# Two attention layers with experts on one core: a reordered start, a later routing, loads and a mask bias moved at the turn between the layers

## The chip, the cores and the metric

The kernel runs on one core of a Trainium2 chip, in float32. Time is what the device takes for one launch, in microseconds (us). It has five engines with a queue of instructions each: TensorE (PE, matrix products and transposes; its loading of weights is listed as PEld), VectorE (DVE), ScalarE (ACT, functions from loaded tables, and copies), GpSimd (POOL) and SyncE (SP, which only issues transfers). Engines wait for each other by semaphores; an instruction that waits holds up all behind it in its own queue.

## The reference

Four batches of 512 rows of 256 values (x), each with a context of 1024 rows. Four steps change x in turn, each on the layer norm of x:

```python
x = x + L0_xattn(layernorm(x), ctx_1024, w_sim, b_sim, W_qv, b_qv)    # similarity attention
x = x + L0_ffn(layernorm(x), gate_w, expert_bias, w1, w2)             # 8 experts + 4 that return x, top 2
x = x + L1_xattn(layernorm(x), ctx_1024, mask, Wq, Wkv, Wo)           # 4 heads of 64
x = x + L1_ffn(layernorm(x), Wg, alpha, ln_w, ln_b, fc1, fc2)         # 8 experts, top 2
```

Layer 0's similarity of row i and context row j is x_i·w1 + c_j·w2 + (x_i·w3)·c_j + b. Its softmax over j weighs the context into one row for each x_i (`hq`); the softmax over i of the row maxima weighs x into one row of the batch (`hc`). The four blocks x, hq, x·hq, x·hc are multiplied by W_qv. An expert layer takes logits of each row, keeps the two largest, and adds the two experts' outputs with the softmax of the two logits as weights.

## The kernel before

**Stages.** Layer 0's attention goes batch by batch; then come the last routing, the keys and values of batches 0 and 1 for layer 1, layer 0's experts, the turn (expert outputs added to x, keys and values of batch 2, queries of batch 0), layer 1's attention in 32 units (four batches, four row tiles, two pairs of heads), and layer 1's experts. PE's order is written out by hand as the functions are called; SP's is so within the expert layers. VectorE, ScalarE and GpSimd get their order from a scheduler that takes priorities and dependencies; a dependency may be added by hand (`after`). Each buffer name belongs to a pool with a fixed number of slots (six of 8 KB, two larger ones, twelve of 4 KB), and a new user of a slot waits for the old.

**Loads (L130 to L169).** SP issues x_0, ctxT_0 (the transposed context), ctxn_0 (the plain one), W_qv, then x and ctxT of batches 1 to 3, then ctxn_1 to ctxn_3. Twelve small constants go by ACT's queue (`small`). Transfers rotate over eight semaphores, so that one waits for the eighth before it. After the last ctxT has landed, GpSimd issues zero fills of the rows and expert-output buffers in memory (L170 to L183, 20.6 MB).

**Layer 0's attention (L241 to L412).** `sim_prep` makes the layer norm of a batch, transposes it, scales it (`q0T`), multiplies it by a row vector (`junk`) and has GpSimd add a bias to x. `sim_scores` makes one row tile's scores, their maximum (VectorE) and exponentials (ScalarE). `turn_probs` divides and transposes the probabilities. `sim_finish` makes the attended product (L295), the reduced row and the product with W_qv, whose first four terms of `weff` close a batch. Into these the scores of the next batch are woven. `route_steps` routes a batch in four steps: norm and transposes, logits, the two largest and their counts (`pos`), then places, at which GpSimd scatters the rows to memory by eight indirect transfers (L753). The steps of batch b stand ahead of the next attended product.

**Layer 0's experts and the turn (L873 to L1031).** `tile_table` works out which expert each tile of 128 rows belongs to; 35 tiles read their rows, go through two products and are stored to `ys`. Then `layer0_experts` makes keys and values of batch 2, loads each batch's two expert outputs into 8 KB buffers (`yb`) and adds them to x on VectorE:

```python
    moe(L0, slots)
    sts[2] = mha_kv(2)
    for b in range(NB):
        y = t8([P, 2, NT, D], f"yb_{b}")
        ...
            nc.vector.tensor_tensor(x[b], y[:, k], x[b], ALU.add)
```

**Layer 1's attention (L418 to L595).** `mha_q` loads the mask of a batch, makes the norm, its transposes and the queries; for batch 0 it runs before the first unit, for the others it is woven into the units of the batch before. `mha_scores` makes the mask's bias (L478) at the first pair of heads of each row tile.

Of the kernel before, what the change touches and what calls it, by code (L numbers as in the profile page):

```python
# [8 lines left out]
F32 = mybir.dt.float32  # L9
# [8 lines left out]
P = 128  # L18
# [25 lines left out]

# [4 lines left out]
def two_layers(ctx: ExitStack, tc: tile.TileContext, io, out):  # L52
# [76 lines left out]

    def small(name, shape, src):  # L130
        t = const.tile(shape, F32, tag=name, name=name)
        nc.scalar.dma_start(out=t, in_=src)
        return t


# [8 lines left out]

    for b in range(NB):
        t = res.tile([P, NT, D], F32, tag=f"x{b}", name=f"x_{b}")
        nc.sync.dma_start(out=t, in_=io["x"][b].rearrange("(t p) d -> p t d", p=P))
        x.append(t)
        if b == 0:
            wsim = small("wsim", [P, 3, NC], io["w_sim"])  # L150
            bsim = small("bsim", [P, 1], io["b_sim"].partition_broadcast(P))
        t = res.tile([P, NC, M], F32, tag=f"ctxT{b}", name=f"ctxT_{b}")
        last_load = nc.sync.dma_start(out=t, in_=io["ctxT"][b].rearrange("(c p) m -> p c m", p=P))
        ctxT.append(t)
        if b == 0:
            load_ctxn(0)
            wqv = t8([P, 8, D], "wqv")
            nc.sync.dma_start(out=wqv, in_=io["W_qv"].rearrange("(k p) d -> p k d", p=P))
    bqv = small("bqv", [P, D], io["b_qv"].partition_broadcast(P))
    wsim_row = small("wsim_row", [P, D], io["w_sim_row"].partition_broadcast(P))  # L160
    gate_w = small("gate_w", [P, NC, ET0], io["gate_wT"].rearrange("(c p) e -> p c e", p=P))
# [23 lines left out]

    def layernorm(src, name):
        st = tsmall([P, NT, 6], "ln_st")
        mv = tsmall([P, NT, 2], "ln_mv")
        for t in range(NT):
            nc.vector.bn_stats(out=st[:, t, :], in_=src[:, t, :])  # L190
            nc.vector.bn_aggr(out=mv[:, t, :], in_=st[:, t, :])
        sd = tsmall([P, NT], "ln_sd")
        nc.scalar.activation(sd, mv[:, :, 1], AF.Sqrt, bias=eps)
        rs = tsmall([P, NT], "ln_rs")
        nc.vector.reciprocal(rs, sd)
        dst = t4([P, NT, D], name)
        for t in range(NT):
            nc.vector.tensor_scalar(
                dst[:, t, :], src[:, t, :], mv[:, t, 0:1], rs[:, t : t + 1], ALU.subtract, ALU.mult
            )  # L200
        return dst
# [38 lines left out]

    def sim_prep(b):  # L241
        xn = layernorm(x[b], f"xn0_{b}")
        eT = t4([P, NC, S], f"eT_{b}")
        qT = t4([P, NC, S], f"q0T_{b}")
        for c, pt in transposed(xn, f"eTp_{b}"):
            nc.vector.tensor_copy(eT[:, c, :], pt)
            nc.vector.tensor_scalar(  # L247
                qT[:, c, :], eT[:, c, :], wsim[:, 2, c : c + 1], wsim[:, 1, c : c + 1], ALU.mult, ALU.add
            )
        negmax = tsmall([P, NT], "s0_negmax")  # L250
        r = tsmall([P, NT], "s0_r")
        for t in range(NT):
            junk = t4([P, D], f"junk_{b}_{t}")
            nc.vector.tensor_tensor_reduce(
                junk, xn[:, t, :], wsim_row, 1.0, 0.0, ALU.mult, ALU.add, r[:, t : t + 1]
            )
        nc.gpsimd.tensor_tensor(x[b], x[b], bqv.unsqueeze(1).to_broadcast([P, NT, D]), ALU.add)
        return dict(b=b, xn=xn, eT=eT, qT=qT, negmax=negmax, r=r)

# [16 lines left out]
    def sim_finish(st):  # L276
# [15 lines left out]
        def attend(c):  # L292
# [5 lines left out]
            nc.scalar.copy(hq[:, c, :], op)  # L298
            nc.vector.tensor_tensor(eh[:, c, :], op, eT[:, c, :], ALU.mult)  # L299

# [59 lines left out]
    def layer0_attention():  # L360


        st, ps, routes = {0: sim_prep(0)}, {}, []

# [3 lines left out]
        def turns(b, t):  # L368
            if t == 0:
                st[b]["aT"] = tbig(f"a0T_{b}")  # L370
            turn_probs(st[b]["aT"], ps.pop(t), t, f"a0t_{b}_{t}")

        load_ctxn(1)
        scores(0, 0)
        scores(0, 1)
        turns(0, 0)
        scores(0, 2)
        turns(0, 1)
        scores(0, 3)
        st[1] = sim_prep(1)  # L380
        turns(0, 2)
        turns(0, 3)
        for b in range(NB):
            more = b + 1 < NB
            fin = sim_finish(st[b])
            next(fin)
            if more:
                scores(b + 1, 0)
            if routes:
                next(routes[-1])  # L390
            next(fin)
            if more:
                scores(b + 1, 1)
# [3 lines left out]
            next(fin)  # L397
            r = route_steps(L0, b)
            routes.append(r)
            next(r)  # L400
            if more:
                scores(b + 1, 2)
                turns(b + 1, 1)
                scores(b + 1, 3)
                if b + 2 < NB:
                    load_ctxn(b + 2)
                    st[b + 2] = sim_prep(b + 2)
                turns(b + 1, 2)
                next(r)
                next(r)  # L410
                turns(b + 1, 3)
                next(r)  # L412
        return r

# [3 lines left out]

    def mha_kv(b):

        kT = ctx_room(0, [P, NC, M], "kT_2") if b == 2 else t8([P, NC, M], f"kT_{b}")
        for n in range(NC):
            for h in range(2):
                op = mm_ps(f"k_{b}_{n}_{h}")
                for c in range(NC):
# [6 lines left out]
                else:  # L432
                    nc.vector.tensor_copy(kT[:, n, bass.ts(h, 512)], op)
        v = ctx_room(1, [P, NJ, D], "v_2") if b == 2 else t8([P, NJ, D], f"v_{b}")
        for g in range(NJ // 2):
            op = mm_ps(f"v_{b}_{g}")
            for k in range(2):
# [8 lines left out]
            else:  # L446
                nc.scalar.copy(d, op)
        return dict(b=b, kT=kT, v=v)

    def mha_q(st):  # L450
        b = st["b"]
        mask = t4([P, NT, M], f"mask_{b}", U8)
        nc.gpsimd.dma_start(out=mask, in_=io["mask"][b].rearrange("(t p) m -> p t m", p=P))
        xn = layernorm(x[b], f"xn2_{b}")
        yield
# [3 lines left out]
        for n in range(NC):  # L459
# [7 lines left out]
            else:  # L467
                nc.scalar.copy(qT[:, n, :], op)
        st.update(qT=qT, mask=mask)
        yield  # L470

    def mha_scores(st, n, t):

        b = st["b"]
        if n == 0:
            if t == 0:
                st["mbias"] = t8([P, NT, M], f"mbias_{b}", BF16)
            nc.vector.tensor_scalar(  # L478
                st["mbias"][:, t, :], st["mask"][:, t, :], 1.0, MASKED, ALU.subtract, ALU.mult
            )  # L480
        sps = [score_ps(f"s2_{b}_{n}_{t}_{r}") for r in range(2)]
# [9 lines left out]
        for r in range(2):  # L491
# [7 lines left out]
            ps.append(p)  # L499
        nc.vector.reciprocal(tot, tot)  # L500
        return ps, tot
# [49 lines left out]
    def layer1_attention(sts):  # L551
# [3 lines left out]
        units = []  # L555
        for _ in mha_q(sts[0]):
            pass
        for b in range(NB):
# [3 lines left out]
        for i in range(len(units) + 4):  # L562
# [22 lines left out]
            if b < NB and i % (2 * NT) == 2:  # L585
                queries = mha_q(sts[b] if b in sts else sts.setdefault(b, mha_kv(b)))
                next(queries)
# [94 lines left out]
    def route_steps(L, b):  # L682
# [49 lines left out]
        pos_i = tsmall([P, 2, NT], "rt_posi", I32)  # L732
        nc.vector.tensor_copy(pos_i, pos)  # L733
        wk = tsmall([P, 2, NT], "rt_wk")
# [30 lines left out]
        if L.n == 0:  # L765
            for t in range(NT):
                xs = x[b][:, t, :]
                nc.vector.scalar_tensor_tensor(xs, xn[:, t, :], wz[:, t : t + 1], xs, ALU.mult, ALU.add)
            yield
# [23 lines left out]
    def tile_table(L):  # L793
# [3 lines left out]
        n = tsmall([P, EX], "tt_n")  # L797
        nc.vector.tensor_tensor(n, lim, base[:, 0:EX], ALU.subtract)
        nc.vector.tensor_scalar(n, n, float(P - 1), None, ALU.add)
# [30 lines left out]
        dl = tsmall([P, EX], "tt_dl")  # L830
        nc.vector.tensor_tensor(dl[:, 0 : EX - 1], lim[:, 1:], lim[:, 0 : EX - 1], ALU.subtract)
        nc.vector.tensor_scalar(dl[:, EX - 1 :], lim[:, EX - 1 :], -1.0, None, ALU.mult)
        nc.vector.tensor_tensor(tmp, past, dl.unsqueeze(1).to_broadcast(big_shape), ALU.mult)
# [38 lines left out]

    def moe(L, slots):  # L873
        nf, n = L.nf, L.n
# [24 lines left out]
        def turn(i):  # L899
# [10 lines left out]
            if n == 0:  # L910
                nc.vector.tensor_copy(hT.rearrange("p c n -> p (c n)"), pt[:, 0:D])  # L911
            else:
# [59 lines left out]
        def run(lo, hi, at=None):  # L972
# [6 lines left out]
            for i in range(lo, hi + 1):  # L979
# [8 lines left out]
                if i > lo:  # L988
                    down(i - 1)
                    if i - 1 + RING < hi:  # L990
                        load_w(i - 1 + RING, 1)
                if i == at:
                    used.append(
# [19 lines left out]
    def layer0_experts(route):  # L1013

        slots = ring_slots(L0)
        sts = {0: mha_kv(0)}
        for _ in route:
            pass
        sts[1] = mha_kv(1)
        moe(L0, slots)  # L1020
        sts[2] = mha_kv(2)
        for b in range(NB):
            y = t8([P, 2, NT, D], f"yb_{b}")
            for k in range(2):
# [4 lines left out]
            for k in range(2):  # L1029
                nc.vector.tensor_tensor(x[b], y[:, k], x[b], ALU.add)  # L1030
        return sts  # L1031
# [82 lines left out]
```

## Time and profile before

| what | us |
|---|---|
| median of 5 runs (1034.93 to 1047.82) | 1045.27 |
| profiled execution, its own time | 1040.41 |
| its span, first to last instruction | 1038.5 |
| PE busy in the span | 916.3 |
| mean granted PE clock, share of full | 0.944 |

| stage | from, us | to, us | PE busy, us |
|---|---|---|---|
| loads and start of layer 0's attention | 0 | 48 | 25.9 |
| layer 0's attention, from the first attended product | 48 | 251 | 185.4 |
| last routing, keys and values of 0 and 1 | 251 | 290 | 33.8 |
| layer 0's experts | 290 | 400 | 106.3 |
| turn to layer 1 | 400 | 436 | 24.8 |
| layer 1's attention, its routing woven in | 436 | 750 | 278.0 |
| layer 1's experts | 750 | 1039 | 262.1 |

A line of the timeline has the start and the duration, the engine, the line of code, the operation, output and input, how often, and in brackets the idle time just before it with what ended it. A line of the waits has the total, the number of times and the longest. The slices cut the span in 40 equal parts and give the busy share of each in tenths. Engines work side by side; PE's gaps are where another engine or a transfer sets the pace.

### The profile page before, as it was taken

To read this page: it belongs to the slowest core of one execution; us is meant where nothing else is said; L and a number is where in the kernel's file an instruction comes from. 1 tells how busy PE (TensorE), PEld (TensorE's weight loads), DVE (VectorE), ACT (ScalarE), POOL (GpSimd) and SP (SyncE) were. 2 spreads that over 40 slices of the span, in tenths; PEclk is the share of its full clock that TensorE was granted. 3 is DMA by queue.
4 is the path that set the end of the run, shared out by engine and by line. 5 is a ranking of instruction groups with operands and counts; after the bars stand their busy time and mean duration, and the time that the engine had idled before them with its cause. 6 is when DMAs were issued, how large, how long until landed. Compare 5 with 4: busy or idle time off the path is not lost.

```text
span 1038.5 us, 15201 instructions
## 1 busy us (share of the span) xinstructions
PE 916.3 (88%) x5506; PEld 679.9 (65%) x5506; DVE 440.0 (42%) x1258; ACT 314.7 (30%) x714; POOL 224.8 (22%) x261
## 2 busy tenths in 40 slices
PE   4797989989899997799999789789669999999994
PEld 1445454646589985457656456566359999999993
DVE  4627466453622222766657256455521112111110
ACT  1212121121121110255655245455212323223230
POOL 2311120303312221010131230330622121222121
PEclk9899999999999998889999899889769999999997
DMA  8999900301068895100000101100624877678963
GB/s 286 303 221 250 272 15 1 110 4 68 28 222 265 247 327 177 66 21 2 21 1 6 56 21 42 41 21 2 258 89 105 253 239 236 178 244 263 305 210 97
DMA packets 55225, 144.65 MB, mean 139 GB/s; under 512 B 6454, under 2 KB 33133, under 8 KB 48968
## 3 DMA queue, kind: packets, MB, share of 16 engines
q1 hardware_dynamic: 37680, 103.90, 29.7%
q0 software_dynamic: 15344, 38.36, 15.1%
q10 hardware_dynamic: 2120, 1.35, 0.4%
q8 instruction: 46, 0.75, 0.3%
q14 instruction: 35, 0.29, 0.1%
HBM read 142.02 MB, written 42.14 MB: 177 GB/s over the span
## 4 chain that ended last, share of the span: by engine, by line
PE 43%; DVE 5%; issue 5%; ACT 3%; DMA 2%; POOL 1%; SPq 0%; POOLq 0%; ACTq 0%; DVEq 0%
PE hp L929 12%; PE y L950 11%; PE s L485 6%; PE a2t L508 4%; PE o L533 3%; DVE p L494 2%; ACT p L498 2%; PE q L462 1%; PE v L439 1%; PE k L426 1%; DMA acc<-yw,to 1%; PE wo L548 1%; DVE mbias L478 1%; ACT a2T L513 1%; POOL rowbuf L671 1%
## 5 line engine op out<-in xcount | busy, mean ns | idle before, releaser
L929 PEld LDWEIGHTS hp<-hT,w1s 128*128 128x128 f32 x1120 | 133.1, 195 | 3.7 <-DVE hT L915 1.9
L929 PE MATMUL hp<-hT,w1s 128*128 128x128 f32 x1120 | 133.7, 279 | 1.3 <-DVE hT L915 1.3
L938 ACT ACTIVATE aT<-hp,w1s 128x128 f32<-128x128 f32 x280 | 76.3, 383 | 168.4 <-issue 168.4
L950 PE MATMUL y<-w2s,aT 128*128 128x256 f32 x560 | 126.5, 379 | 0.0
L950 PEld LDWEIGHTS y<-w2s,aT 128*128 128x128 f32 x560 | 103.7, 190 | 12.7
L494 DVE CUSTOM_DVE_ANT_0 p<-s,mbias 128x1024 f32<-128x1024 f32 x64 | 75.8, 1221 | 71.7 <-PE s L485 71.7
L967 POOL DMA_INDIRECT acc<-yw,to x35 | 54.2, 1548 | 211.9 <-DVE to L902 126.9
L498 ACT ACTIVATE p<-p,s_nm 128x1024 f32<-128x1024 f32 x64 | 73.4, 1148 | 71.8 <-DVE s_nm L494 71.8
L508 PEld LDWEIGHTS a2t<-ident,p 128*128 128x128 f32 x512 | 58.3, 146 | 53.5 <-issue 34.3
L508 PE MATMUL a2t<-ident,p 128*128 128x128 f32 x512 | 73.6, 288 | 19.8 <-issue 12.2
L753 POOL DMA_INDIRECT rows<-rowbuf,rt_posi x64 | 63.2, 988 | 123.0 <-DVE rt_posi L733 88.0
L954 DVE TENSOR_SCALAR yw<-y,row 128x256 f32<-128x256 f32 x63 | 30.5, 484 | 135.2 <-PE y L950 135.2
L485 PE MATMUL s<-kT,q2T 64*128 64x512 f32 x256 | 72.3, 667 | 1.4 <-DVE s_nm L494 1.4
L915 DVE TENSOR_SCALAR hT<-ht,w1s 128x128 f32<-128x128 f32 x70 | 25.5, 406 | 95.1 <-PE ht L909 88.8
L533 PE MATMUL o<-a2T,v 128*64 128x128 f32 x1024 | 63.3, 276 | 0.0
L530 POOL COPY s_rs<-s_tot 128x128 f32<-128x128 f32 x32 | 9.8, 307 | 237.6 <-DVE s_tot L500 171.6
L533 PEld LDWEIGHTS o<-a2T,v 128*64 128x64 f32 x1024 | 55.4, 137 | 7.9 <-issue 7.3
L265 PE MATMUL s<-ctxT,q0T 128*128 128x512 f32 x128 | 59.2, 607 | 1.4 <-DVE q0T L247 1.4
L295 PE MATMUL hq<-a0T,ctxn 128*128 128x512 f32 x128 | 58.2, 609 | 0.9 <-DVE ehT L299 0.9
L513 ACT COPY a2T<-a2t 128x512 f32<-128x512 f32 x96 | 53.0, 582 | 15.7 <-PE a2t L508 14.5
L929 PEld LDWEIGHTS hp<-hT,w0s 128*128 128x128 f32 x448 | 54.3, 192 | 3.2 <-DVE hT L911 1.8
L929 PE MATMUL hp<-hT,w0s 128*128 128x128 f32 x448 | 54.7, 275 | 1.4 <-DVE hT L911 1.4
(222 smaller groups left out, 1205.8 us busy)
## 6 DMA issues: line engine op xcount, KB each, us to landing
w1s<-in_w1p SPq DMA_DIRECT2D x38, 1030.0 KB
w2s<-in_w2p SPq DMA_DIRECT2D x38, 1024.0 KB
rows<-zeros POOLq DMA_DIRECT2D x8, 2064.0 KB
w0s<-in_w1p SPq DMA_DIRECT2D x31, 512.0 KB
w0s<-in_w2p SPq DMA_DIRECT2D x31, 512.0 KB
row<-rows SPq DMA_DIRECT2D x63, 129.0 KB
ctxT<-in_ctxT SPq DMA_DIRECT2D x4, 1024.0 KB
ctxn<-in_ctx SPq DMA_DIRECT2D x4, 1024.0 KB
```

The costliest lines, as they stand in the source:

```text
L265: nc.tensor.matmul(sp[:, h, :], st["qT"][:, c, bass.ts(t, P)], ctxT[b][:, c, bass.ts(h, 512)], start=(c == 0), stop=(c == NC - 1),)
L295: nc.tensor.matmul(op, ctxn[b][:, j, bass.ts(c, P)], aT[:, j, :], start=(j == 0), stop=(j == NJ - 1))
L485: nc.tensor.matmul(sps[r][:, k, :], st["qT"][at, n, bass.ts(t, P)], st["kT"][at, n, bass.ts(k, 512)], start=True, stop=True,)
L494: nc.vector.tensor_tensor_reduce(p, sps[r].rearrange("p h n -> p (h n)"), st["mbias"][:, t, :], -ATT_SCALE, -ATT_SCALE * LEAST, ALU.add, A ...
L498: nc.scalar.activation(p, p, AF.Exp, bias=nm, scale=-1.0, accum_out=tot[:, r : r + 1])
L508: nc.tensor.transpose(pt[:, bass.ts(j, P)], p[:, bass.ts(4 * g + j, P)], ident)
L513: nc.scalar.copy(d, pt)
L533: nc.tensor.matmul(op[r * HD : r * HD + HD, :], st["v"][:, j, bass.ts(2 * n + r, HD)], aT[:, r, bass.ts(j, P)], start=(j == 0), stop=(j == ...
L753: i = nc.gpsimd.indirect_dma_start(out=rows[:, :], out_offset=bass.IndirectOffsetOnAxis(ap=pos_i[:, k, t : t + 1], axis=0), in_=buf[:, k, ...
L929: nc.tensor.matmul(o, w1[:, c * ff + f * P : c * ff + f * P + P], hT[:, c, :], start=(c == 0), stop=(c == NC - 1),)
L938: nc.scalar.activation(aT[:, f, :], hp[:, f // 4, bass.ts(f % 4, P)], AF.Gelu_apprx_tanh, bias=w1[:, at : at + 1])
L950: nc.tensor.matmul(op, aT[:, f, :], w2[:, f * D : f * D + D], start=(f == 0), stop=(f == nf - 1))
```

## The change

It has five parts.

1. The start. A square root of a constant is run on ScalarE ahead of all, which loads its table. Only two small loads stay on ACT's queue, two go to GpSimd's, and eight to SP's, behind the last ctxT and ahead of ctxn_1 to ctxn_3. SP's order becomes x_0, ctxT_0, x_1, ctxn_0, W_qv, ctxT_1, and so on.
2. `sim_prep` is cut in three: the norm, the transposes with the scaling, the products with the row vector. The norm of batch 1 is put behind batch 0's scaling, those of 2 and 3 behind the attended product two batches before.
3. The routing of a batch is taken one batch later, step by step among the next batch's products. Batch 3's is woven into the keys and values of 0 and 1 by `AMONG`: so many parts of these ahead of each step. The x updates and the tile table are put behind the places.
4. The mask of batch 0 is loaded ahead of layer 0's experts, and its four biases are made among their tiles, from the eighth on.
5. At the turn all eight expert outputs are loaded into the two large buffers. x_0's adds stay on VectorE, behind the last key copy of batch 2; the other six go to GpSimd. Queries of batch 0 come in the code right after x_0's adds. The norms of the other batches are put behind a unit's reciprocal.

```diff
+AMONG = (2, 1, 1, 2, 0)
...
-    def small(name, shape, src):
+    def small(name, shape, src, queue=nc.sync):
         t = const.tile(shape, F32, tag=name, name=name)
-        nc.scalar.dma_start(out=t, in_=src)
+        queue.dma_start(out=t, in_=src)
         return t
+    nc.scalar.activation(const.tile([P, 1], F32, tag="root", name="root"), eps, AF.Sqrt, bias=eps)
...
+    load_x(0)
+    wsim = small("wsim", [P, 3, NC], io["w_sim"], nc.scalar)
+    bsim = small("bsim", [P, 1], io["b_sim"].partition_broadcast(P), nc.scalar)
+    bqv = small("bqv", [P, D], io["b_qv"].partition_broadcast(P), nc.gpsimd)
+    wsim_row = small("wsim_row", [P, D], io["w_sim_row"].partition_broadcast(P), nc.gpsimd)
+    load_ctxT(0)
+    load_x(1)
+    load_ctxn(0)
+    wqv = t8([P, 8, D], "wqv")
+    nc.sync.dma_start(out=wqv, in_=io["W_qv"].rearrange("(k p) d -> p k d", p=P))
+    load_ctxT(1)
+    for b in range(2, NB):
+        load_x(b)
+        last_load = load_ctxT(b)
...
-    def layernorm(src, name):
+    def layernorm(src, name, behind=None):
...
-            nc.vector.bn_stats(out=st[:, t, :], in_=src[:, t, :])
+            i = nc.vector.bn_stats(out=st[:, t, :], in_=src[:, t, :])
+            if behind is not None:
+                after(i, behind, "a transfer does not hold up what VectorE has to do before")
...
+    def sim_norm(b, behind=None):
+        return dict(b=b, xn=layernorm(x[b], f"xn0_{b}", behind))
...
         for b in range(NB):
             more = b + 1 < NB
             fin = sim_finish(st[b])
             next(fin)
+            if b + 2 < NB:
+                st[b + 2] = sim_norm(b + 2, st[b]["attended"])
+            step()
             if more:
                 scores(b + 1, 0)
-            if routes:
-                next(routes[-1])
             next(fin)
+            step()
             if more:
                 scores(b + 1, 1)
             next(fin)
             if more:
                 turns(b + 1, 0)
             next(fin)
-            r = route_steps(L0, b)
-            routes.append(r)
-            next(r)
+            step()
             if more:
+                sim_rows(st[b + 1])
                 scores(b + 1, 2)
                 turns(b + 1, 1)
                 scores(b + 1, 3)
                 if b + 2 < NB:
                     load_ctxn(b + 2)
-                    st[b + 2] = sim_prep(b + 2)
+                    sim_prep(st[b + 2])
+            step()
+            if more:
                 turns(b + 1, 2)
-                next(r)
-                next(r)
                 turns(b + 1, 3)
-                next(r)
-        return r
+            route = route_steps(L0, b)
+            next(route)
+        return route
...
-        sts = {0: mha_kv(0)}
-        for _ in route:
+        mask = mha_mask(0)
+        def biases():
+            for t in range(NT):
+                after(mha_bias(sts[0], t), L0.turned, "a transfer does not hold up the tiles")
+                yield
+        sts = {}
+        kvs = mha_kvs(sts, (0, 1))
+        for n in AMONG:
+            for _ in range(n):
+                next(kvs)
+            next(route, None)
+        for _ in kvs:
             pass
-        sts[1] = mha_kv(1)
-        moe(L0, slots)
-        sts[2] = mha_kv(2)
+        sts[0]["mask"] = mask
+        moe(L0, slots, biases())
+        for _ in mha_kvs(sts, (2,)):
+            pass
         for b in range(NB):
-            y = t8([P, 2, NT, D], f"yb_{b}")
+            if b % 2 == 0:
+                yb = tbig(f"yb_{b}").rearrange("p (b k t) (w d) -> p b k (t w) d", b=2, k=2, d=D)
+            y = yb[:, b % 2]
...
             for k in range(2):
-                nc.vector.tensor_tensor(x[b], y[:, k], x[b], ALU.add)
+                if b == 0:
+                    i = nc.vector.tensor_tensor(x[b], y[:, k], x[b], ALU.add)
+                    after(i, sts[2]["copied"], "a transfer does not hold up the copies of the keys")
+                else:
+                    nc.gpsimd.tensor_tensor(x[b], y[:, k], x[b], ALU.add)
+            if b == 0:
+                for _ in mha_q(sts[0]):
+                    pass
```

## The prediction

> **What bounds the kernel now.** I read the page's busy shares and slices first, then PE's idle by stage, then the rows at each gap, last the chain of waits.
>
> ```profile
> PE 916.3 (88%) x5506; PEld 679.9 (65%) x5506; DVE 440.0 (42%) x1258; ACT 314.7 (30%) x714; POOL 224.8 (22%) x261
> PE   4797989989899997799999789789669999999994
> DVE  4627466453622222766657256455521112111110
> ```
>
> PE sets the pace in nearly all slices, so only PE's gaps can be won. By stage (PE busy of length): 25.9 of 48 us before the first attended product, 185.4 of 203 in layer 0's attention, 33.8 of 39 in the last routing, 106.3 of 110 in layer 0's experts, 24.8 of 36 at the turn to layer 1, 278 of 314 in layer 1's attention, 262 of 289 in its experts. The change edits the first five and hardly the last two.
>
> What holds PE at the start (waits, then rows of ACT and VectorE, then of PE):
>
> ```profile
> PE eTp L208 <- DVE xn L198: 17.5, 4, 13.7
> DVE ln_st L190 <- DMA x<-in_x: 8.1, 2, 5.0
> ```
> ```profile
> 10.73 0.48 ACTq L132 DMA_DIRECT2D wo<-in_Wo  x1
> 11.30 1.28 ACT L193 ACT_TABLE_LOAD   x1 [11.30 <-DMA alpha<-in_alpha]
> 12.60 0.30 ACT L193 ACTIVATE ln_sd<-ln_mv,eps 128x4 f32<-128x4 f32 x1
> ```
> ```profile
> 22.74 0.75 DVE L190 BATCH_NORM_STATS2 ln_st<-x 128x6 f32<-128x256 f32 x2 [3.07 <-DMA x<-in_x]
> 24.95 2.40 DVE L271 TENSOR_REDUCE s_negmax<-s 128x1 f32<-128x1024 f32 x2
> ```
>
> x_0's statistics are done at 6.7, but the square root waits until ACT has issued its 12 loads (to 11.2) and loaded its table. Later VectorE stands before x_1, while the first scores (ready from 21) wait for their maximum.
>
> At the last routing and the turn PE waits as follows:
>
> ```profile
> 272.53 0.42 PE L719 MATMUL pos<-rt_cnt,before 128*128 128x48 f32 x2 [3.19 <-DVE rt_cnt L711]
> ...
> 411.19 3.78 PE L426 MATMUL k<-ctxT,wkv 128*128 128x512 f32 x4 [5.00 <-DVE kT L433]
> 414.77 7.99 PE L439 MATMUL v<-wkv,ctxT 128*128 128x256 f32 x32
> 428.14 2.30 PE L208 MATMUL xn2Tp<-ident,xn 128*128 128x128 f32 x8 [5.38 <-DVE xn L198]
> 430.38 5.33 PE L462 MATMUL q<-xn2T,wq 128*128 128x512 f32 x8
> 435.63 1.99 PE L485 MATMUL s<-kT,q2T 64*128 64x512 f32 x8
> ```
>
> There eight adds of 1.22 us stand in VectorE's queue: the first (409.31) ahead of a key copy that PE needs, the others ahead of query 0's norm.
>
> **Part by part.** *Start.* With two small loads left on ACT and the table loaded beforehand, the root can follow the statistics: 6.7 instead of 12.6, so 5.9 earlier; xn and the first transposes move by as much (13.7 to about 7.9). The score matmuls then need ctxT_0, the second load in either order. VectorE no longer stops at x_1: the wait is put behind batch 0's scaling, and x_1 is issued third, without the stop at 11.16. PE has 3.8 us of gaps at transposes of batch 1 (2.23, 0.75, 0.81), of which I count 2. The first attended product moves from 48.2 to about 40: **−8**. Better end −12 (5.9, all 3.8 and the 2.4 of PE's wait for the first probabilities); worse −5, if the cold clock and later waits take the gaps back (the same 16 score matmuls took 8.79 first and 7.03 later).
>
> *Middle (48 to 251).* The table loads stay as many per batch here; what moves is routing. From a batch's reduced product to the next attended one takes 29.5, 28.4 and 24.9 us. In the first PE stands 2.65 + 0.66 + 0.35 + 0.68 + 0.29 = 4.6 us, the first two for the next norm, which now is made during the attended product, where VectorE waits anyway (21 us idle ahead of L299 from 100 to 260). Batch 0's routing work (2.23 transposes, 2.58 logits, 0.41 back, slow clock) leaves it: about −6.5, the gaps shrinking by only 1.3 because VectorE then has eT, q0T, probabilities and a0T copies in a row. Batch 1: −4.2 (3.3 of routing at full clock, 0.9 of gaps); batch 2: −1.8, since VectorE's four x updates now stand ahead of its last copy (about 1.6). The routing comes back in the next batch's attended stretch: 3.3 less the 1.1 of gaps that it fills (0.35 + 0.77 before the reduced product) is +2.1 twice, and +1.1 in batch 3, where 0.8 of counting moves out. Sum **−7**, from −12 (all the norm's gaps) to 0 (VectorE paces PE).
>
> *Last routing.* Batch 2's count now stands here too, and behind hcq_3 its top-2 has little PE work to hide it: a gap like the 3.19 above, some 4.5 with the logits' copies. Against it, batch 3's same gap is filled by K/V of batch 1. Scatters of 3 (8 at 1.28 on POOL) start when its places are ready, about 24 us behind hcq_3 as now, and batch 2's 8 (10.2 us) have gone before. First expert tile **+2.3** (−2 if K/V covers both, +5 if the clock also falls).
>
> *Experts of layer 0.* Four mask biases of 0.68 go among tiles of 3.7 us on a VectorE with 30.5 of 110 us busy; the mask keeps one small buffer of twelve. **+0.5** (0 to +4; the upper end is a tile's wait for a buffer).
>
> *Turn.* The first yb lands at 409.3 as now; x_0's two adds then end at 411.8, the norm (four statistics 1.7, root 0.3, table 1.28, xn 1.38) by about 416. PE has keys without the 5.0 gap until 407.8 and values until 415.8, so the transposes start near 416, queries near 418.3, scores near 423.7 instead of 435.63: −12, and I take **−11.5**. All eight yb loads still take SP's queue 12.5 us, but x_1 to x_3 are off the path for units of 6.5 us. The six adds on POOL (2.35 each by the 128x1024 row) are 14 us on an engine with 1.8 of 36 busy. They can collide:
>
> ```profile
> 15.82 1.42 DVE L247 TENSOR_SCALAR q0T<-eT,wsim 128x512 f32<-128x512 f32 x1
> ...
> 18.10 0.54 DVE L247 TENSOR_SCALAR q0T<-eT,wsim 128x512 f32<-128x512 f32 x1
> ```
>
> The first ran beside POOL's 128x1024 add (14.61 to 16.96), the second alone. If xn's four likewise take 2.6 times 1.38, it is +2.2: end −8 with a second such copy; other end −14 (no clock loss).
>
> The Trainium skill, "SBUF — State Buffer", section "Who interferes with whom", speaks against this move: GpSimd and VectorE share one port pair, and one of the two blocks for the other's whole instruction. The two rows agree. By the rule a copy could wait out a whole add, a little more than 2.35 us; the sum would be 1.2 us worse than with the 1.42 row.
>
> *Layer 1's attention.* The norms of 1 to 3 are put behind a unit's reciprocal, which by the built program means ten more table loads in the whole. Six to eight lie here, at
>
> ```profile
> 24.84 1.28 ACT L222 ACT_TABLE_LOAD   x1
> 26.18 1.11 ACT L222 ACTIVATE p<-s,s_negmax 128x1024 f32<-128x1024 f32 x1
> ```
>
> 1.28 + 0.06 us each, about 10 us of ACT, in units of which ACT fills half (155.9 of 314). I count a quarter as seen by PE: **+2.5** (0 to +8). The Trainium skill, "ScalarE: Activation LUTs", section "What ACT_TABLE_LOAD costs", has 1.28 plus a drain, 2.66 us a switch; here the next activation follows 0.06 after the load, so this trace shows no drain behind it. By the rule the same quarter would be +5.
>
> **The sum.** −8 −7 +2.3 +0.5 −11.5 +2.5 = −21.2. From the profiled run's own 1040.4 (span 1038.5 and 1.9 around it) that is 1019; from the median 1045.3, which is 4.9 above it, 1024. The profiled run is an ordinary one of the spread (1034.9 to 1047.8), so I say **1022**. Layer 1's experts (750 to 1040) keep order and work.
>
> **Rivals.** *Gain at the turn alone.* If in layer 0 VectorE (102 of 203 us busy, bunched in each batch's second half) becomes PE's bound, starting sooner only means waiting later: −8 + 5 + 2 − 11.5 + 3 = about −9, time 1034. For it: PE's gaps in the middle name VectorE. Against: VectorE is half idle there.
>
> *The turn's adds collide.* POOL's adds slow x_0's norm and first copies: turn −5 rather than −11.5, sum −15, time 1028.
>
> *Starved context loads: slower.* The SP queue now has eight small loads ahead of three contexts, all behind ctxT_3, whose landing releases 20.6 MB of zero fills on POOL's queue. Before, the third context was issued late:
>
> ```profile
> 22.80 45.24 SPq L142 DMA_DIRECT2D ctxn<-in_ctx  x3
> ```
>
> It was issued at 68, moved 0.06 MB by 75, then 0.25 MB per 5 us until 95: 27 us for 1 MB beside fills. Batch 1's attended product (near 84 now) needs context 1. Up to 4 MB at 50 GB/s from about 29 end at 109, context 1 at about 70, batch 2's by 90 (needed near 135). It decides if the rate falls below about 35 GB/s: at half the 50, context 1 lands near 110, PE stands 26 us and the sum is +5; with nothing until the fills end (about 120) it is +15. Time 1048 to 1058. For it: that 7 us with 0.06 MB. Against: 0.25 MB per 5 us after it.
>
> *It doesn't do what it says*: the gaps stay because another wait ends last at the same place (ctxT_0's landing at the start, yb's at the turn); about −3, time 1041.
>
> **How the numbers follow.** Forecast (−13 to −32) 0.68; gain at the turn alone 0.14; collision 0.07; starved 0.07; not as said 0.04. Range 1009 to 1038: the low end has the middle's and the start's better ends with the sum's others, the high end takes in the first two rivals and the worse ends of middle and layer 1. A measurement here tells about 1%, 10.5 us: faster 0.68 + 0.06 + 0.06 = 0.80; within 1% 0.13 (rest of those two, and the last); slower 0.07.
>
> **What would show it.** Right: the first root at about 6.8, first attended product near 40; fewer than 2 us at transposes per batch; no 5.0 gap in kT and scores about 24 us after the last expert product instead of 36. Wrong: PE waiting for ctxn in batch 1 or 2; a gap over 5 us before counting; xn of query 0 over 3 us; more PE idle in units with a table load; first tile over 5 us later behind hcq_3.

## The result, and the profile after

The changed kernel takes 1042.1 us (median of 44 runs) against 1041.6 for the kernel before (86 runs); the ratio is 1.0002, 95% interval 0.999 to 1.0014. No change can be seen, where 2% less was forecast. The start did move, and most of what it won was lost again before layer 1's attention began.

The page of the changed kernel, its busy shares and two of its slices:

```profile
PE 923.0 (88%) x5506; PEld 683.4 (65%) x5506; DVE 441.1 (42%) x1252; ACT 328.1 (31%) x725; POOL 240.5 (23%) x269
PE   5888989898898999689889799799669999999994
DVE  6454563725623223565656356456531111211110
```

PE is busier at once (5 and three 8s for 4, 7, 9, 7), and no busier afterwards. By stages, in us. They are split at the small product that stands right ahead of the first attended one, at the end of the last product with W_qv, at the first expert tile's transposes, at the end of the last expert product, at the first score, and at the end of layer 1's last attention output. The last columns are g_all, the repaired kernel of the third group below; each column is one traced run, and g_all's is from another chip:

| stage | before | predicted step | after | step | repaired | step |
|---|---|---|---|---|---|---|
| to the first attended product | 48.1 | −8 | 39.5 | −8.6 | 38.8 | −9.3 |
| rest of layer 0's attention | 203.1 | −7 | 206.9 | +3.8 | 197.1 | −6.0 |
| last routing to first expert tile | 38.1 | +2.3 | 42.0 | +3.9 | 39.7 | +1.6 |
| layer 0's experts | 110.2 | +0.5 | 112.8 | +2.6 | 110.4 | +0.2 |
| turn, to the first score | 36.0 | −11.5 | 31.9 | −4.1 | 21.7 | −14.3 |
| layer 1's attention, to its last output | 298.0 | +2.5 | 304.8 | +6.8 | 303.0 | +5.0 |
| the rest of the span | 304.9 | 0 | 305.9 | +1.0 | 305.4 | +0.5 |
| span | 1038.5 | −21.2 | 1043.8 | +5.3 | 1016.1 | −22.4 |

The profiled run of after is 3.6 us above its median (1045.6 with what stands around the span), that of before 1.2 below its own; the stages say where time went, and the medians how much in all.

PE's rows at the start, at the weights of batch 0 and of batch 1, and at the last routing (start, duration, what, and in brackets the idle time before with its releaser):

```profile
7.61 2.21 PE L223 MATMUL eTp<-ident,xn 128*128 128x128 f32 x8 [7.61 <-DVE xn L213]
...
39.70 8.36 PE L317 MATMUL hq<-a0T,ctxn 128*128 128x512 f32 x16
...
74.30 2.93 PE L353 MATMUL hcq<-weff,eT 128*128 128x256 f32 x6 [3.20 <-DVE weff L371]
...
131.05 0.98 PE L365 MATMUL hcc<-ones,b_hr 1*128 1x1 f32 x4 [2.53 <-DVE a0T L251]
...
250.59 0.66 PE L771 MATMUL pos<-rt_cnt,before 128*128 128x48 f32 x2 [3.87 <-DVE rt_cnt L763]
...
284.84 3.72 PE L475 MATMUL v<-wkv,ctxT 128*128 128x256 f32 x16 [2.14 <-DVE v L481]
```

The first transposes come at 7.61 (13.70 before), the first attended product at 39.70 (48.23): the start is as forecast. The gaps at 74.30, 131.05 and 284.84 are new. Behind them stand these rows: of VectorE at weff (the kernel before, then after) with GpSimd's beside it, of ACT at the exponential of batch 2's second row tile, of VectorE at the first tiles' row numbers.

```profile
78.65 0.88 DVE L349 SCALAR_TENSOR_TENSOR weff<-wqv,b_hc 128x256 f32<-128x256 f32 x2
```
```profile
69.87 4.38 DVE L371 SCALAR_TENSOR_TENSOR weff<-wqv,b_hc 128x256 f32<-128x256 f32 x2
69.92 1.65 POOL L192 DMA_DIRECT2D ys<-zeros  x1 [20.56 <-issue]
71.51 2.42 POOL L268 TENSOR_TENSOR x<-x,bqv 128x1024 f32<-128x1024 f32 x1
```
```profile
128.00 1.11 ACT L237 ACTIVATE p<-s,s_negmax 128x1024 f32<-128x1024 f32 x1 [10.70 <-DMA ys<-zeros]
```
```profile
283.97 0.22 DVE L958 SCALAR_TENSOR_TENSOR to<-row,tt_valid,tt_aside 128x1 int32<-128x1 f32 x1 [3.98 <-DMA row<-rows]
284.10 0.69 DVE L481 COPY v<-v 128x512 f32<-128x512 f32 x1
```

Two steps of weff took 0.88 us before and 4.38 now: GpSimd issued the fill of ys from 69.92 and added to x_2 from 71.51 to 73.93. The exponential waits for the zero fills to end: they read a constant tile of zeros out of a 4 KB buffer, and that buffer is the one that the exponential is given. And the copy of values that PE needs stands behind a row number whose row is still on its way.

The turn (PE, then VectorE's norm of query 0 before and after, then GpSimd):

```profile
402.54 7.10 PE L461 MATMUL k<-ctxT,wkv 128*128 128x512 f32 x16 [1.32 <-PEq L1063]
409.49 7.30 PE L475 MATMUL v<-wkv,ctxT 128*128 128x256 f32 x32
419.15 0.33 PE L223 MATMUL xn2Tp<-ident,xn 128*128 128x128 f32 x1 [2.37 <-DVE xn L213]
421.50 0.48 PE L223 MATMUL xn2Tp<-ident,xn 128*128 128x128 f32 x1 [2.02 <-DVE xn L213]
423.92 0.47 PE L223 MATMUL xn2Tp<-ident,xn 128*128 128x128 f32 x1 [1.94 <-DVE xn L213]
426.27 1.33 PE L223 MATMUL xn2Tp<-ident,xn 128*128 128x128 f32 x5 [1.87 <-DVE xn L213]
```
```profile
427.67 1.38 DVE L198 TENSOR_SCALAR xn<-x,ln_mv,ln_rs 128x256 f32<-128x256 f32 x4
```
```profile
417.04 9.17 DVE L213 TENSOR_SCALAR xn<-x,ln_mv,ln_rs 128x256 f32<-128x256 f32 x4
```
```profile
414.18 14.31 POOL L1107 TENSOR_TENSOR x<-yb,x 128x1024 f32<-128x1024 f32 x6 [11.18 <-DMA yb<-ys]
```

The gap of 5.0 in the keys is gone, as forecast. But the four steps of xn, 1.38 us before, take 9.17 beside the six adds that went to GpSimd, and PE gets its four row tiles some 2.4 us apart, one for each add.

### The profile page after: what moved, and what is told of

Its sections match the earlier page's. It is cut to its first block, busy times and chain, and to the rows that moved or that the text cites. A ratio compares the mean times of both kernels' runs of the same rounds, so it can differ in the third digit from the quotient of the medians.

```text
span 1043.8 us, 15228 instructions
## 1 busy us (share of the span) xinstructions
PE 923.0 (88%) x5506; PEld 683.4 (65%) x5506; DVE 441.1 (42%) x1252; ACT 328.1 (31%) x725; POOL 240.5 (23%) x269
## 4 chain that ended last, share of the span: by engine, by line
PE 61%; issue 11%; DVE 10%; DMA 8%; ACT 4%; POOL 4%; another core or an unknown queue 1%; SPq 0%; POOLq 0%; DVEq 0%; ACTq 0%
PE hp L985 11%; PE y L1006 10%; PE s L536 6%; PE hq L317 6%; PE s L287 5%; DMA acc<-yw,to 5%; PE a2t L559 4%; PE hcq L353 4%; PE o L584 3%; DVE p L545 2%; ACT p L549 2%; DMA row<-rows 1%; POOL rows L805 1%; POOL ys L1013 1%
## 5 line engine op out<-in xcount | busy, mean ns | idle before, releaser
L559 PEld LDWEIGHTS a2t<-ident,p 128*128 128x128 f32 x512 | 58.7, 147 | 55.4 <-issue 32.5
L536 PE MATMUL s<-kT,q2T 64*128 64x512 f32 x256 | 75.7, 695 | 1.4 <-DVE s_nm L545 1.4
L317 PE MATMUL hq<-a0T,ctxn 128*128 128x512 f32 x128 | 60.3, 627 | 0.0
```

Of the source, the lines that this page charges most:

```text
L317: nc.tensor.matmul(op, ctxn[b][:, j, bass.ts(c, P)], aT[:, j, :], start=(j == 0), stop=(j == NJ - 1))
L536: nc.tensor.matmul(sps[r][:, k, :], st["qT"][at, n, bass.ts(t, P)], st["kT"][at, n, bass.ts(k, 512)], start=True, stop=True,)
L559: nc.tensor.transpose(pt[:, bass.ts(j, P)], p[:, bass.ts(4 * g + j, P)], ident)
```

## The experiments

The runs came in three groups ("calls" in the recorded expectations), each on one chip. The kernel before takes between 1027 and 1041 us on these chips, so a ratio is compared only with those of its own group.

**First group: repair one collision at a time.** The four kernels are the changed one with these edits:

```diff
 f_turn: the adds of x_1 to x_3 behind query 0's norm
-                    nc.gpsimd.tensor_tensor(x[b], y[:, k], x[b], ALU.add)
+                    i = nc.gpsimd.tensor_tensor(x[b], y[:, k], x[b], ALU.add)
+                    after(i, normed["last"], "the first norm goes before")
 f_weff: the fill of ys and the add to x_{b+2} behind batch b's weff
+        after(late_fill["ys"], behind, "the product's weights go before")
+        if behind is not None:
+            after(i, behind, "the product's weights go before")
 f_zeros: the zeros in their own buffer (room for it from one shared in time with oT)
-    zeros = t4([P, ROW], "zeros")
+    zeros = const.tile([P, ROW], F32, tag="zeros", name="zeros")
 f_all: all of these, and the first two tiles' row numbers behind batch 1's values
+            if n == 0 and i < 2:
+                after(k, hold, "the values go before")
```

> The changed kernel, with the six adds on GpSimd put behind the last tile of query 0's norm. Theory (the adds shut VectorE out): xn of query 0 falls from 9.17 us to about 1.4, the first score follows the last expert product by about 24 us instead of 31.9, and the whole is 7 to 8 us faster than the changed kernel, so near 1034. Rival (GpSimd's adds only slow what is bound by the landing of yb): xn is short, but the first score moves by less than 2 us and the time stays within 2 us of 1042. A second rival: the adds now meet the first units, and 3 us or more of the gain come back there.

> The changed kernel, with the fill of ys and the add to x_2 on GpSimd put behind the weights of batch 0's last products (weff). Theory (the same lock, met because the earlier start brings weff under a GpSimd stretch whose time the fills set): weff's two steps fall from 4.38 us to about 0.9, PE's gap of 3.19 at 74.3 goes and the products behind it run at full clock; 4 to 6 us faster than the changed kernel up to batch 1's attended product. Rival (VectorE paces the batch anyway): the gap goes, but the attended product of batch 1 moves by less than 2 us.

> The changed kernel, with the zeros that the fills read in a buffer of their own, so that no exponential waits for the fills' end to get theirs. Theory (the fills' end at about 128 holds ACT for 10.7 us ahead of p of batch 2): PE's gap of 2.53 at 131 goes, and with the slow clock behind it 2 to 4 us in all, in batch 1. Rival (something else of the fills holds VectorE or ACT next): the gap only changes its place, less than 1 us.

> The changed kernel with all three, and the first tiles' row numbers on VectorE put behind the last copy of batch 1's values (they stood ahead of it, waiting for rows, and PE had a gap of 2.13 at 284.8). Theory: the gains add up, 7.8 + 5 + 3 + 2 = about 17 us, time near 1025, the first expert product's gap gone. Rival (the middle is paced by VectorE and the clock): only the turn's part remains, near 1034.

Measured, against 1027.1 us for the kernel before on that chip: f_turn 1006.1 (ratio 0.980, 0.974 to 0.987), f_weff 1015.4 (0.988, 0.982 to 0.995), f_zeros 1016.2 (0.987, 0.981 to 0.993), f_all 1001.3 (0.974, 0.968 to 0.980). On f_turn's VectorE and PE the turn is as the theory had it:

```profile
408.52 1.38 DVE L215 TENSOR_SCALAR xn<-x,ln_mv,ln_rs 128x256 f32<-128x256 f32 x4
```

The first score comes 21.5 us after the last expert product, for 31.9 in after and an expected 24; the adds meet the first units without PE losing more there (layer 1's attention takes 284.7 us, for 289.1 and 287.2 in f_weff and f_zeros). In f_weff the two steps of weff take 0.88 us and PE's wait at them is 0.77 for 3.20; the attended product of batch 1 follows that of batch 0 by 52.5 us and not 58.4. All four gained more than was expected: 11 to 26 us on the kernel before, for 2 to 17 on the changed one. What a repair is worth in the whole this group can't tell, for the changed kernel itself was not among the four. And this chip was a poor place for the question of f_zeros: the fills end by 120 here, and in f_weff the exponential still waited for them (8.52 us) without PE losing time.

**Second group: the changed kernel and the one before on one chip, and parts alone.**

> The changed kernel itself, once more, on the chip of the other runs of this call. The four kernels of the first call ran on a chip on which the kernel before took 1027 us and not 1042. If the changed kernel is worth the same everywhere, its ratio to the kernel before is 1.000 here too; if the waits for instructions (6.45 and 5.7 us in the two traces) and the fills' times differ by chip, the two ratios differ, and by the repaired kernels of the first call (0.987 to 0.988 with one repair of 4 to 6 us each) it would be 0.992 to 0.994.

> The kernel before itself, for a trace from the same chip as the others of this call. Its stages should be those of the first trace (48, 203, 38, 110, 36 us up to the first score); if this chip is the quick one, layer 1's attention is about 10 us shorter than 298, without PE's two waits for instructions.

b_start is the kernel before with the first part alone (loads and table). a_noturn is the changed kernel with its turn put back (batch 0's queries too are called ahead of the units again, in lines not shown):

```diff
-                yb = tbig(f"yb_{b}").rearrange("p (b k t) (w d) -> p b k (t w) d", b=2, k=2, d=D)
-            y = yb[:, b % 2]
+            y = t8([P, 2, NT, D], f"yb_{b}")
...
-                    nc.gpsimd.tensor_tensor(x[b], y[:, k], x[b], ALU.add)
+                nc.vector.tensor_tensor(x[b], y[:, k], x[b], ALU.add)
...
-                queries = mha_q(sts[b], sts[b - 1]["unit"])
+                queries = mha_q(sts[b])
```

> The kernel before with the first part of the change alone: order and queues of the loads, and the square root's table ahead. By the prediction's first step the first attended product moves from 48.2 to about 40 and the whole is 8 us faster (ratio 0.992). Rival (an earlier start only meets the fills on GpSimd, which stay where they were): the attended product is earlier, but weff of batch 0 stands 2 to 3 us under GpSimd's add and half of the gain or more is given back before batch 3: ratio 0.996 or more.

> The changed kernel with the turn and the norms of layer 1 as before: eight adds on VectorE, yb in the 8 KB buffers, norms not put behind a unit (the early mask bias stays). By the traces the turn loses the 4 us that the change won there (32 to 36), and layer 1's attention wins back what the extra table loads cost, 2 to 7 us. Theory (the turn's part as changed is worth about nothing): ratio to the changed kernel 0.997 to 1.002. Rival (the turn as changed is still a gain, and layer 1's longer time only chance): 4 us slower than the changed kernel, 1.004.

Measured, against 1026.9: c_after 1029.9 (1.0033, 1.0007 to 1.0058), c_before 1029.0 in its one run, b_start 1025.9 (0.9998, 0.9976 to 1.0021), a_noturn 1025.0 (0.998, 0.996 to 0.9999).

So the changed kernel is no better on this chip, and the 0.992 to 0.994 that the first group would have given was wrong. The reason is one stretch, from batch 1's attended product to batch 2's: 66.9 us, for 59.1 in c_before. ACT's row and PE's in c_after:

```profile
129.29 1.11 ACT L237 ACTIVATE p<-s,s_negmax 128x1024 f32<-128x1024 f32 x1 [19.23 <-DMA ys<-zeros]
```
```profile
132.34 1.01 PE L365 MATMUL hcc<-ones,b_hr 1*128 1x1 f32 x4 [11.06 <-DVE a0T L251]
```

In the first trace the same wait cost PE only 2.53 us, because weff's collision had already made batch 1 late; here weff met no GpSimd add, and the whole start ran into the wait. In the first trace of the kernel before the same exponential came by itself when the fills had ended:

```profile
131.76 1.11 ACT L222 ACTIVATE p<-s,s_negmax 128x1024 f32<-128x1024 f32 x1 [4.23 <-DVE s_negmax L271]
```

The first part alone (b_start) moves the attended product only from 50.0 to 46.6, not by 8. VectorE shows why: with the loads in the new order it stands before x_1's statistics, ahead of x_0's norm, and the first transposes come at 14.20 as in the kernel before.

```profile
11.99 0.75 DVE L201 BATCH_NORM_STATS2 ln_st<-x 128x6 f32<-128x256 f32 x2 [5.00 <-DMA x<-in_x]
```

So the start's 8 us need the second part too, which puts x_1's norm behind the scaling. That b_start's time is the rival's is not the rival's doing: its weff takes 0.88 us. Where its 3.4 us go isn't shown; in the two traces it is still 5.0 us ahead of c_before at the first expert tile, while the medians differ by 1.0, with an interval that leaves room for a gain of 2.5.

a_noturn is 4.9 us faster than c_after in the medians (0.998 and 1.0033, intervals apart): the turn's part as changed costs time, more than the theory allowed (at most 3 us). Its turn takes 26.3 us for 30.4 in c_after and 35.6 in c_before, with all eight adds on VectorE and the old gap in the keys:

```profile
415.12 3.44 PE L461 MATMUL k<-ctxT,wkv 128*128 128x512 f32 x4 [4.62 <-DVE kT L468]
```

Why a_noturn's turn is 9.3 us shorter than c_before's shows in SP's loads of the expert outputs (c_before, then a_noturn):

```profile
408.23 12.48 SPq L1026 DMA_DIRECT2D yb<-ys  x8
```
```profile
409.26 22.44 SPq L1099 DMA_DIRECT2D yb<-ys  x8
```

The loads are spread out, so that only four of the eight adds are ready before query 0's norm is done; in c_before all eight (1.22 us each) and two mask biases (0.67 each) stand ahead of it, and PE waits 5.38 us for it, in a_noturn not at all. The later loads go with the early mask bias, which now holds one of the six 8 KB buffers that the expert outputs use too; that this is the reason is likely, not tested. So the bias may have helped as much by holding the buffer as by having been made earlier, and the adds' move to GpSimd was not needed for this gain. Layer 1's attention takes 282.5 us in c_before, 282.9 in c_after and 283.0 in a_noturn. ACT has 14 table loads there in c_after and 8 in the other two: the further loads cost nothing that shows on this chip, and the 2 to 7 us that a_noturn was expected to win back there were not to be had.

**Third group: is the fills' end a wall?** Here the changed kernel stands beside the repairs; g_nozeros is g_all (that is, f_all) with the zeros left where they were.

> The changed kernel again, as the base of the three kernels beside it on one chip. Theory (a wall): the exponential of batch 2's second row tile waits until the zero fills have ended, since the zeros' buffer is the next free one; where the fills end at 128 to 130 us PE loses 2 to 11 us in batch 1 (in the two traces so far the stretch from batch 1's attended product to batch 2's took 59.5 and 66.9, and 55.3 on the chip where they end at 120). Ratio to the kernel before 1.000 to 1.003.

> The changed kernel with the zeros in a buffer of their own. Theory (the fills' end is the wall that takes the earlier start back): the stretch of batch 1 is 55 to 56 us wherever the fills end, and the whole 4 to 11 us faster than the changed kernel where they end at 128 or later, about 1 where they end at 120. Rival (the exponential is late for another reason, or VectorE waits next for the same fills): stretch of batch 1 above 59, less than 2 us faster.

> The changed kernel with the adds of the turn behind query 0's norm, weff ahead of GpSimd's fill and add, and the first row numbers behind the values' copies, but with the zeros where they were. Theory: weff's 3 to 5 us are taken back at the wall where the fills end at 128 or later, so that only the turn (about 9) and the values' copies (2 to 4) count: 11 to 13 us faster than the changed kernel. Rival (no wall): 16 to 18 us faster, as with all four.

> All four repairs. Theory: start, middle and turn then come as predicted, and the ratio to the kernel before is 0.973 to 0.982 on any chip (it was 0.974 on the one of the first call). Rival (the first call's chip alone gave it, where the fills end early): 0.990.

| kernel | us, median | ratio to before (1040.8) | batch 1's stretch | turn |
|---|---|---|---|---|
| g_after | 1045.1 | 1.0041 (1.0024 to 1.0057) | 68.8 | 32.5 |
| g_zeros | 1032.0 | 0.9909 (0.9879 to 0.9940) | 54.2 | 31.7 |
| g_nozeros | 1031.6 | 0.9904 (0.9871 to 0.9938) | 69.7 | 21.9 |
| g_all | 1015.2 | 0.9759 (0.9727 to 0.9790) | 55.3 | 21.7 |

ACT's row of g_after and PE's behind it, then the same two of g_all:

```profile
130.82 1.11 ACT L237 ACTIVATE p<-s,s_negmax 128x1024 f32<-128x1024 f32 x1 [18.81 <-DMA ys<-zeros]
...
133.87 1.01 PE L365 MATMUL hcc<-ones,b_hr 1*128 1x1 f32 x4 [10.64 <-DVE a0T L251]
```
```profile
118.06 1.11 ACT L243 ACTIVATE p<-s,s_negmax 128x1024 f32<-128x1024 f32 x1 [6.18 <-DVE s_negmax L301]
...
123.45 0.60 PE L373 MATMUL hcc<-ones,b_hr 1*128 1x1 f32 x4 [0.35 <-DVE a0T L257]
```

With the zeros in a buffer of their own, 13.0 us are won, more than the 4 to 11 that I had expected, though nothing else is touched but a small row that makes room for it. Left where they were, they cost 16.4 us to a kernel that has all other repairs. Coming sooner doesn't help: batch 0's stretch is 52.6 us in g_nozeros, and batch 1's then has 12.39 us of idle PE at the wall. (In g_after weff met no add either, and batch 0's stretch is 52.6 there too; in g_zeros it did, 4.42 us, and the stretch is 58.6.) The three other repairs bring 13.5 us without the zeros' and 16.8 with it. The sizes of g_nozeros and g_all came within 1 us of what was expected.

## Why the prediction was wrong

The mechanism of the start held: the root is done at once, VectorE doesn't stand before x_1, and −8 was −8.6. It takes both halves of that step: in b_start the loads and the table alone leave the first transposes where they were. (One row was misread there: 7.03 us belongs to sixteen attended products, and eight scores at full speed take 3.60.)

**The step that failed most is the middle, −7.** It measured +3.8, outside its range of −12 to 0. I took one by one the waits that go and asked what comes late next among VectorE's copies. I didn't ask which buffers are still held by something that keeps its own time. By stretches from one attended product to the next, as changes in us against the first trace of the kernel before:

| stretch of | forecast | after | g_after | g_all |
|---|---|---|---|---|
| batch 0 | −6.5 | −2.1 | −7.9 | −7.9 |
| batch 1 | −2.1 | +1.4 | +10.6 | −2.8 |
| batch 2 | +0.3 | +0.5 | +0.7 | +0.6 |
| batch 3, to the last product with W_qv | +1.1 | +4.0 | +4.1 | +4.1 |

*Batch 1.* The exponential of batch 2's second tile gets the buffer of the zeros, which the fills read until 128 to 131. In the trace of before it ran at 131.76, when VectorE's maximum was there, and the wait cost nothing. Whatever comes some 3 us sooner meets it. The start's 8 us and the middle's own could therefore not pass that point: PE reaches the weights of batch 1 at 132.8 in the first trace and at 135.7 in g_after, for 138.5 before, however early it started. Without the wait the stretch is −2.8 and the whole middle −6.0 (g_all).

*Batch 0.* Here weff is late. Moving it from 78.65 to 69.87 brought it under GpSimd's fill of ys and the add behind it. It took 4.38 us in after, 4.42 in g_zeros and 0.88 in g_after: where the fill falls decides, by less than a microsecond (issued at 69.92, 70.23 and 70.72). The fill itself seems to be timed by the earlier fills: where nothing was put ahead of it, it is issued at 66.3 and 67.1 on the chip where the fills end at 120 (f_zeros, f_turn), and at 68.6 to 71.4 on the others.

*Batch 3.* The step was priced too low in every trace. The first half of its attended product took 8.95 us at a granted clock of 0.78, for 7.03 at 1.00 before. The routing's products, which then stood right ahead of it, are gone from there, and PE has gaps of 2.89 and 0.68 us instead; that these lowered the clock is likely, not tested.

"Starved context loads" had the right transfers in mind, and the wrong thing behind them: PE waits for no context in any trace of the changed kernel or its repairs, and the fills held a buffer instead. "Gain at the turn alone" had the right course, a start that only means waiting later, but named VectorE's bunching as the cause; and little of the gain at the turn was there either.

**The turn, −11.5, failed by the price of the lock.** It measured −4.1. The −11.5 counted nothing for GpSimd's adds beside the norm. They were priced at +2.2, as one end of the range, and as a rival, "The turn's adds collide", with −5 for the turn; this rival's course is what came, as did the sign "xn of query 0 over 3 us". The row that I used (1.42 us beside GpSimd, 0.54 alone) is one copy beside one add, and I took the four steps of xn as one such copy. They are four, and the six adds stand back to back: each step waits for a whole add (9.17 us; four adds of 2.35 are 9.4), +7.8 in all. The Trainium skill, "SBUF — State Buffer", section "Who interferes with whom", says that the later of the two blocks for the other's whole instruction. The trace agrees, and the error was mine: I applied its rule to one copy and not to each step. Not all of VectorE's work is held so: beside the same adds the statistics take 0.40 us each and the copies of PE's results 0.66 to 0.69, as elsewhere. Behind the norm (f_turn) xn takes 1.38 again, and in g_all the whole turn is −14.3. The gap in the keys, which the forecast put first, is not all of the gain: a_noturn has it still (4.62), and a turn of 26.3.

**Last routing, +2.3.** The exposed count is there (3.87, expected 4.5). What I missed is VectorE's queue: row numbers that wait for a row stood ahead of the copy of values, 2.14 us. With that mended the step is +1.6.

**Experts, +0.5, and layer 1's attention, +2.5.** The bias among the tiles costs nothing that shows: 110.2 in g_after, as before; the 2.6 of the first trace are waits for row loads (5.0 us in all, for 1.3 in g_after and 1.6 before). The attention was +6.8, +3.9 and +0.4 in three traces of the changed kernel against the kernel before, the last on a chip with both traces. That the table loads cost the others' excess isn't shown. The Trainium skill, "ScalarE: Activation LUTs", section "What ACT_TABLE_LOAD costs", adds a drain to each; in the trace of after the next activation starts 0.01 us behind the load:

```profile
456.11 1.28 ACT L549 ACT_TABLE_LOAD   x1
457.40 1.15 ACT L549 ACTIVATE p<-p,s_nm 128x1024 f32<-128x1024 f32 x1
```

The repaired stages add up to −22.4 where −21.2 was forecast, and g_all's median, 1015, lies in the range that the changed kernel missed. That the sums come so near is in part luck: the turn won 2.8 us more than forecast, the start 1.3, and the attention lost 2.5 more. And g_all is not the kernel that was forecast.

## What to carry to other kernels

Before counting a gain, list what keeps its own time (a long transfer started early, an engine that works through a queue behind it) and ask of each step that moves forward whether it now needs a buffer, an engine or a port that this holds. A buffer that comes free just before it is needed shows no wait in the trace of before; a step that moves forward by a few microseconds then stands at it as at a wall. When work is moved to GpSimd, price it by each of VectorE's steps beside it that it can hold up, here one whole add for each step of xn, and put it behind the short steps that a path needs. The two repairs that paid here are small: a buffer of its own for a constant that transfers read, and a dependency by hand on the last step of the norm.

## What the runs showed of the hardware

The same kernel takes 1027 us on some chips and 1041 on others. Two things differ in the traces. In PE's rows of layer 1's attention the slow ones show two waits that no engine ends:

```profile
580.37 1.12 PE L508 MATMUL a2t<-ident,p 128*128 128x128 f32 x4 [6.45 <-issue]
...
671.13 1.12 PE L508 MATMUL a2t<-ident,p 128*128 128x128 f32 x4 [5.71 <-issue]
```

They (4.9 to 6.5 us each) are in the first traces of both kernels and in the four of the third group; the eight traces of the first two groups lack them, and their layer 1 attention takes 280 to 289 us for 298 to 305. An expectation calls them waits for instructions; no run shows that, and what PE waits for there isn't settled. And the zero fills end at 120 in the first group's traces, at 128 to 131 in those of the others. A kernel whose order leans on when a transfer ends can so lose time on one chip and not on another: with the same wait for the fills, batch 1's stretch is 55.3 us in f_weff and 69.7 in g_nozeros.

I had also not expected that short steps beside a row of long GpSimd adds get just one turn between two adds: xn's four came out 2.4 us apart, as long as an add, though each is 0.35 us by itself.
